# Sums and differences stored side by side in groups of four images, with matching loads and output, and the poles' rows loaded over 128 partitions

## The chip, the cores and the metric

The kernel runs on one core of a Trainium2 chip. The metric is device time in microseconds for one launch. The core has a matrix engine (TensorE, in the profile PE, with its weight loads as PEld), a vector engine (DVE), a scalar engine (ACT), a general engine (POOL) and a synchronisation engine (SP), which here issues nearly all transfers. Transfers between the on-chip memory and DRAM are carried out by 16 DMA engines.

## The reference

The input `x` has 16 images of 16 channels, 256 by 256, in float32. Two layers follow each other, each adding its result to its input:

```python
    # --- layer 0 (conv_preact) ---
    x = x + _L0_conv_ref(_gn(x), L0_conv_weight)
    # --- layer 1 (conv_preact) ---
    x = x + _L1_conv_ref(_gn(x), L1_conv_ty, L1_conv_tx, L1_conv_weights_pole1, L1_conv_weights_pole2, L1_conv_weights_residue)
    return x
```

`_gn` is a normalisation over 8 groups of two channels. Layer 0 is a circular 3 by 3 convolution of the 16 channels, which the reference writes with Fourier transforms. Layer 1 is a product in the Fourier domain with weights built from poles and residues, followed by two inverses:

```python
        alpha = jnp.fft.fft2(x, axes=(-2, -1))
        ...
        A = 1.0 / (omega1[:, None, None, None] - weights_pole1[None])
        Bm = 1.0 / (omega2[:, None, None, None] - weights_pole2[None])
        S = jnp.einsum('ikpq,oikp,xikq->oxik', weights_residue, A, Bm)
        output_residue1 = jnp.einsum('biox,oxik->bkox', alpha, S)
        C = jnp.einsum('biox,oikp->bikpx', alpha, A)
        D = jnp.einsum('bikpx,xikq->bikpq', C, Bm)
        output_residue2 = jnp.einsum('bikpq,ikpq->bkpq', D, weights_residue)
        x1 = jnp.fft.ifft2(output_residue1, s=(Ny, Nx), axes=(-2, -1)).real
        ...
        return x1 + x2 / Nx / Ny
```

`x2` is the transient: exponentials of the poles along both axes, weighted with `output_residue2`.

## The kernel before

The work is done in four stages, one after the other, with two tensors between them in DRAM that matter here: `v`, the result of layer 0, and the spectra. `v` is not kept as rows but as sums and differences of mirrored rows: for each row y of the upper half and its mirror image 255 - y, `vD[b][0]` holds the sum and `vD[b][1]` the difference, as 128 half rows by 16 channels by 256 columns, one tensor for each of the 16 images.

*Convolution* (lines 280 to 322). One image is 24 steps of `conv(g)`, and 384 steps follow each other. A step issues 16 matmuls of 32 by 32 weights. Six steps make a unit `u`, a quarter of an image: the accumulators of rows `r` 0 and 1 (upper half) are evicted by ACT at its last step (line 309), those of the mirrored rows, `r` 2 and 3, three steps later, each pair into a buffer `vt` of 4 KB per partition, of which there are six. Two steps on, `mirror` (line 259) forms the sum on DVE into `vsum` (two buffers, line 261) and the difference on POOL in place (line 264), and puts on lists what follows: ACT squares both for the statistics of layer 1 (line 272), and SP stores them (line 319), the sum's two halves at steps +4 and +5 and the difference's at +6 and +7 counted from the second eviction. A store has 256 KB, in runs of 1 KB. The rows of `x` are loaded two images ahead (line 123), in parts, on the same SP queue, and DVE takes their moments (line 179).

Between these steps the tables of layer 1 are made, one `yield` per step, by the generators `make_coef`, `make_poles`, `make_hat(0)`, `make_hat(1)` and `make_c`. `make_poles` computes seven quantities for all poles and writes each as 16 equal rows of 1024 numbers into `hD`. `make_hat` (line 419) needs five of them in all 128 partitions, in two halves of 512 numbers for each of two sides, four sets in all. It loads a set with eight transfers (line 439), each of five quantities from the 16 rows of `hD` to 16 partitions, waits six steps, and then ACT squares two of them (lines 452, 453), before POOL, DVE and PE go on.

*Transform* (lines 726 to 895). For each channel `i` and each group of four images from `b0`, `load_v` (line 726) reads sums and differences of the four images into a tile `s` of 2 by 4 by 256 numbers in each of 128 partitions, with one transfer per image; `fold` mirrors once more along x on DVE and POOL; PE transforms along y (lines 762, 770) and x (line 805). The loads run two groups ahead; the first group's is issued by POOL, the others by SP.

*Mixing* (lines 898 to 1228) reads the spectra `aD`, multiplies with the weights, and writes `yD`. It does not touch `v`.

*Inverse* (lines 1231 to 1426). 64 units of one channel `k` and four images. `load_v` (line 1281) reads the same parts of `v` again into `vl` (two buffers), one transfer per image; `combine` (POOL, line 1301) prepares the spectrum `yk`; PE goes along x (line 1337) and y (lines 1361, 1362); DVE writes the result into `r`. One unit later `put_out` (line 1368) adds half of `vl` to `r`, forms sum (line 1372) and difference (line 1373) of the two halves, which are the rows of the upper half and their mirror images, and stores each as one transfer for four images (line 1375).

Every transfer issued by SP waits until the one eight places before it on SP has landed, since eight semaphores are used in turn.

Of the kernel before, what the change touches and what calls it, by code (L numbers as in the profile page):

```python
# [9 lines left out]
FP = mybir.dt.float32  # L10
AF = mybir.ActivationFunctionType
ALU = mybir.AluOpType
# [4 lines left out]
B = 16  # L17
C = 16
N = 256
P = 128  # L20
# [4 lines left out]
def conv_then_laplace_kernel(ctx: ExitStack, tc: tile.TileContext, a: dict, out: bass.AP):  # L25
# [15 lines left out]
    nc = tc.nc  # L41
    x = a["x"]
# [22 lines left out]

    vD = [dp.tile([2, P, C, N], FP, name=f"vD{b}", tag=f"vD{b}") for b in range(B)]
    aD = dp.tile([P, 2 * C, N * B], FP, name="aD", tag="aD")
# [39 lines left out]
    p1 = ExitStack()  # L107
    wp = p1.enter_context(tc.tile_pool(name="conv_w", bufs=1))
    xp = p1.enter_context(tc.tile_pool(name="xt", bufs=5))
    vp = p1.enter_context(tc.tile_pool(name="vt", bufs=6))  # L110
    fp = p1.enter_context(tc.tile_pool(name="v_sums", bufs=2))
    jp = p1.enter_context(tc.tile_pool(name="junk", bufs=1))
# [145 lines left out]

    def mirror(g, b, u, lo, hi):
        both = fp.tile([P, 2, 2, N], FP, name="vsum", tag="vsum")  # L260
        nc.vector.scalar_tensor_tensor(  # L261
            both, lo, 1.0, hi, ALU.mult, ALU.add, accum_out=sums[:, b, u : u + 1]
        )
        nc.gpsimd.tensor_tensor(lo, lo, hi, ALU.subtract)  # L264
        folded.extend((g + 4 + 2 * j + r, b, u, j, t, r) for j, t in enumerate((both, lo)) for r in range(2))
        squared.append((g + 5, lambda: square(both, 4 + 2 * u, b, bias=shift2[:, b : b + 1])))
        squared.append((g + 7, lambda: square(lo, 5 + 2 * u, b)))

    def square(t, col, b, **by):

        junk = jp.tile([P, 4 * N], FP, name="junk", tag="junk")
        nc.scalar.activation(
            junk,
            t.rearrange("p r j x -> p (r j x)"),
            AF.Square,
            accum_out=sums[:, b, col : col + 1],
            **by,
        )

    def conv(g):  # L280
# [20 lines left out]
        for r in (0, 1) if g % 6 == 5 else (2, 3) if g % 6 == 2 else ():  # L301
            at = g if r < 2 else g - 3
            if not 0 <= at < 24 * B:
                continue
            b, u = at // 24, at // 6 % 4
            if r % 2 == 0:
                vt = vp.tile([P, 2, 2, N], FP, name="vt", tag="vt")
                acc["v", r // 2] = vt
            nc.scalar.activation(vt[:, r % 2], acc[r], AF.Identity, bias=ready[b][1])  # L309
            if r == 3:  # L310
                later.append((g + 2, lambda g=g, b=b, u=u, lo=acc["v", 0], hi=vt: mirror(g, b, u, lo, hi)))
        while later and (later[0][0] <= g or g >= 24 * B + 2):
# [3 lines left out]
        while folded and (folded[0][0] <= g or g >= 24 * B + 2):  # L316
            _, b, u, j, t, r = folded.pop(0)
            y = 64 * r + 16 * u
            nc.sync.dma_start(
                out=vD[b][j, y : y + 16].rearrange("(t y) c x -> (y c) t x", t=2),  # L320
                in_=t[:, r],
            )
# [96 lines left out]
    def make_hat(side):  # L419
# [12 lines left out]
        n = C * C * 2  # L432
        for half in range(2):
# [3 lines left out]
            at = slice(half * n, half * n + n)  # L437
            for p0 in range(0, P, 16):
                nc.sync.dma_start(
                    out=five[p0 : p0 + 16, 0:5],  # L440
                    in_=hD[0:5, side, :, at].rearrange("j a n -> a j n"),
                )
# [283 lines left out]
    def load_v(i, b0, eng=nc.sync):  # L726
        s = sp.tile([P, 2, 4, N], FP, name="s", tag="s")
        for j in range(4):
            eng.dma_start(
                out=s[:, :, j], in_=vD[b0 + j][:, :, i, :].rearrange("h y x -> y h x")  # L730
            )
        return s

# [547 lines left out]
    def load_v(k, b0):  # L1281
        vl = vp.tile([P, 2, 4, N], FP, name="vl", tag="vl")
        for j in range(4):
            nc.sync.dma_start(
                out=vl[:, :, j], in_=vD[b0 + j][:, :, k, :].rearrange("h y x -> y h x")
            )
        return vl
# [80 lines left out]
    def put_out(k, b0, r, vl):  # L1368

        nc.vector.scalar_tensor_tensor(r, vl, 0.5, r, ALU.mult, ALU.add)  # L1370
        ol = op.tile([P, 2, 4, N], FP, name="ol", tag="ol")
        nc.vector.tensor_tensor(ol[:, 0], r[:, 0], r[:, 1], ALU.add)
        nc.vector.tensor_tensor(ol[:, 1], r[:, 0], r[:, 1], ALU.subtract)
        for h in range(2):
            nc.sync.dma_start(
                out=out[k, b0 : b0 + 4, h].rearrange("b y x -> y b x"), in_=ol[:, h]
            )

# [23 lines left out]
    for n, (k, b0) in enumerate(units):  # L1402
# [7 lines left out]
        if n + 1 < len(units):  # L1410
# [4 lines left out]
            load_ahead(n + 1)  # L1415
        r = rp.tile([P, 2, 4, N], FP, name="r", tag="r")
        for j in range(4):
            pt = along_x(u_now[:, j])
            if last is not None:
                along_y(*last)  # L1420
            if j == 0 and n:
                put_out(*done)
            last = (ey_now[:, j], hs[:, j], pt, r[:, :, j], begun[j])
        done = (k, b0, r, v_now)
# [160 lines left out]
```

## Time and profile before

| | |
|---|---|
| median of 6 runs | 2675.11 us (2671.88 to 2684.48) |
| the profiled execution | 2671.88 us, span 2669.8 us |
| PE, PEld busy | 2485.9 us (93%), 1872.1 us (70%) |
| DVE busy | 1988.4 us (74%) |
| ACT busy | 1447.8 us (54%) |
| POOL busy | 1311.1 us (49%) |
| moved by DMA | 653.17 MB, mean 245 GB/s |
| packets | 476827, of them 426998 under 2 KB |
| issues: stores of v | 256 of 256 KB |
| issues: loads of v | 256 and 256 of 256 KB |
| issues: output | 128 of 512 KB |
| issues: poles' rows | 32 of 160 KB |

The span runs from the first to the last instruction. Busy times of engines overlap, so they don't add up to it. A share of busy time is a mean over four stages with different limits. The granted clock is the share of full speed at which TensorE was allowed to run; the DMA share is the mean busy share of the 16 DMA engines, and in a short window it can come out a little above 1. In a row of the timeline, what stands in brackets is how long the engine was idle before the instruction, and what ended that.

### The profile page before, as it was taken

To read this page: it belongs to the slowest core of one execution; us is meant where nothing else is said; L and a number is where in the kernel's file an instruction comes from. 1 tells how busy PE (TensorE), PEld (TensorE's weight loads), DVE (VectorE), ACT (ScalarE), POOL (GpSimd) and SP (SyncE) were. 2 spreads that over 40 slices of the span, in tenths; PEclk is the share of its full clock that TensorE was granted. 3 is DMA by queue.
4 is the path that set the end of the run, shared out by engine and by line. 5 is a ranking of instruction groups with operands and counts; after the bars stand their busy time and mean duration, and the time that the engine had idled before them with its cause. 6 is when DMAs were issued, how large, how long until landed. Compare 5 with 4: busy or idle time off the path is not lost.

```text
span 2669.8 us, 84449 instructions
## 1 busy us (share of the span) xinstructions
PE 2485.9 (93%) x35314; PEld 1872.1 (70%) x35314; DVE 1988.4 (74%) x3805; ACT 1447.8 (54%) x2726; POOL 1311.1 (49%) x1182
## 2 busy tenths in 40 slices
PE   5888999879999999997999999999699999999998
PEld 2454444457777777774877777788588888888887
DVE  7767688748888888887777778787366666766666
ACT  2565566566666666664666666666244444444443
POOL 1333368343333333333566755766546565555653
PEclk9999999989999999997999999999899999999999
DMA  7898979765656655664777777777889998898985
GB/s 273 276 277 277 285 254 307 259 207 174 217 202 229 237 211 200 237 237 149 216 223 225 225 222 223 219 226 221 243 274 296 285 289 284 282 292 280 298 277 180
DMA packets 476827, 653.17 MB, mean 245 GB/s; under 512 B 51062, under 2 KB 426998, under 8 KB 466592
## 3 DMA queue, kind: packets, MB, share of 16 engines
q1 hardware_dynamic: 475376, 640.58, 74.7%
q8 instruction: 278, 4.55, 0.7%
q0 software_dynamic: 928, 3.02, 0.4%
q10 hardware_dynamic: 144, 4.19, 0.4%
q14 instruction: 101, 0.83, 0.1%
HBM read 368.15 MB, written 280.36 MB: 243 GB/s over the span
## 4 chain that ended last, share of the span: by engine, by line
PE 55%; DMA 17%; DVE 14%; SPq 6%; ACT 3%; issue 3%; POOL 2%; ACTq 0%; DVEq 0%; POOLq 0%
PE ps_conv L294 11%; PE ps_y L762 9%; PE ps_y L770 8%; PE ps_mix L1094 7%; DMA yk<-yD 6%; DMA yD<-yt 6%; PE ps_x L805 4%; PE ps_p L1337 3%; PE ps_f L1361 3%; PE ps_f L1362 3%; DVE r L1370 3%; SPq L1108 3%; DMA out_y<-ol 3%; PE ps_s L1012 2%; DVE xst L179 2%
## 5 line engine op out<-in xcount | busy, mean ns | idle before, releaser
L1094 PE MATMUL ps_mix<-abd,sg 128*64 128x128 f32 x8192 | 480.1, 275 | 40.3 <-ACT yt L1207 29.4
L1094 PEld LDWEIGHTS ps_mix<-abd,sg 128*64 128x64 f32 x8192 | 446.2, 137 | 97.4 <-ACT yt L1207 54.7
L1301 POOL TENSOR_TENSOR u<-yk 128x512 f32<-128x512 f32 (+1 forms) x268 | 345.6, 1320 | 307.0 <-PE ps_p L1337 200.8
L294 PE MATMUL ps_conv<-xt,wc 32*32 32x512 f32 x12288 | 447.9, 612 | 46.8 <-issue 36.0
L294 PEld LDWEIGHTS ps_conv<-xt,wc 32*32 32x32 f32 x12288 | 249.4, 104 | 233.6 <-issue 146.6
L778 ACT ACTIVATE t<-ps_y,vmr 128x384 f32<-128x384 f32 x512 | 297.5, 581 | 162.9 <-PE ps_y L770 162.8
L1028 DVE STREAM_SHUFFLE sg<-ps_s 128x512 f32<-128x512 f32 (+1 forms) x264 | 326.0, 1325 | 0.0
L762 PE MATMUL ps_y<-tabE,vq 128*128 128x256 f32 x1024 | 313.5, 388 | 13.4 <-DVE vq L751 11.9
L264 POOL TENSOR_TENSOR vt<-vt 128x1024 f32<-128x1024 f32 x64 | 151.7, 2370 | 324.9 <-DVE vsum L261 256.4
L770 PE MATMUL ps_y<-tabO,vq 128*128 128x256 f32 x1024 | 306.0, 381 | 0.0
L1337 PEld LDWEIGHTS ps_p<-inv,u 128*128 128x128 f32 x2048 | 265.9, 193 | 50.4 <-issue 25.1
L1361 PE MATMUL ps_f<-pt,inv 128*128 128x256 f32 x1008 | 300.8, 380 | 0.0
L1362 PE MATMUL ps_f<-hs,ey 128*128 128x256 f32 x1008 | 299.8, 379 | 0.0
L1365 DVE TENSOR_TENSOR r<-ps_f,q 128x256 f32<-128x256 f32 x256 | 107.1, 419 | 252.9 <-ACT q L1364 252.9
L1337 PE MATMUL ps_p<-inv,u 128*128 128x128 f32 x2048 | 279.3, 280 | 13.3 <-POOL u L1305 13.1
L1207 ACT COPY yt<-ps_mix 128x512 f32<-128x512 f32 x352 | 191.1, 593 | 156.8 <-DMA yD<-yt 105.8
L309 ACT ACTIVATE vt<-ps_conv,xq 128x512 f32<-128x512 f32 x256 | 162.1, 683 | 167.6 <-PE ps_conv L294 167.4
L762 PEld LDWEIGHTS ps_y<-tabE,vq 128*128 128x128 f32 x1024 | 189.7, 191 | 89.9 <-ACT q L818 50.3
L1364 ACT COPY q<-ps_f 128x256 f32<-128x256 f32 x256 | 95.4, 373 | 288.8 <-PE ps_f L1362 283.8
L750 POOL TENSOR_TENSOR vq<-vf 128x512 f32<-128x512 f32 x64 | 81.5, 1273 | 293.4 <-DVE vf L754 276.5
L1339 ACT COPY pt<-ps_p 128x512 f32<-128x512 f32 x256 | 150.2, 587 | 136.4 <-PE ps_p L1337 132.0
L770 PEld LDWEIGHTS ps_y<-tabO,vq 128*128 128x128 f32 x1024 | 195.7, 191 | 27.0
(239 smaller groups left out, 4062.5 us busy)
## 6 DMA issues: line engine op xcount, KB each, us to landing
yD<-yt SPq DMA_DIRECT2D x512, 128.0 KB, 3.5
vl<-vD SPq DMA_DIRECT2D x256, 256.0 KB, 3.9
out_y<-ol SPq DMA_DIRECT2D x128, 512.0 KB, 9.6
s<-vD SPq DMA_DIRECT2D x252, 256.0 KB, 5.8
aD<-spec SPq DMA_DIRECT2D x15, 4096.0 KB, 13.5
yk<-yD SPq DMA_DIRECT2D x60, 1024.0 KB, 8.5
xt<-in_x SPq DMA_DIRECT2D x64, 645.0 KB, 5.9
xt<-in_x SPq DMA_DIRECT2D x64, 516.0 KB, 6.9
```

Source lines behind the costliest of these rows:

```text
L294: nc.tensor.matmul(acc[r][32 * c : 32 * c + 32], lhsT=ready[b][0][rows, phase, tap], rhs=halves[b][u // 2][rows, q : q + 5 : 4, 2 - tap : ...
L309: nc.scalar.activation(vt[:, r % 2], acc[r], AF.Identity, bias=ready[b][1])
L762: nc.tensor.matmul(ps[:, 0:N], lhsT=vf[:, xo, 0, j], rhs=tabE[:, 0 : i + 2 : i + 1], start=True, stop=False, skip_group_check=True,)
L770: nc.tensor.matmul(ps[:, P : P + N], lhsT=vf[:, xo, 1, j], rhs=tabO[:, i : C + 1 : C - i], start=False, stop=True, skip_group_check=True,)
L778: nc.scalar.activation(t[:, xo, j].rearrange("p l n -> p (l n)"), ps[:, 0:384], AF.Copy, scale=vmr[:, 0, b0 + j, i : i + 1],)
L1028: nc.vector.stream_shuffle(to[..., C + k : C + k + 2], src, swap)
L1094: nc.tensor.matmul(ps[64 * t : 64 * t + 64, j], lhsT=sg[:, f : f + 2].rearrange("p f m -> p (f m)"), rhs=abd[jq][:, :, 2 * t + cc, 2 * jj ...
L1207: (nc.vector.tensor_copy if m >= (2 if late else 3) else nc.scalar.copy)(o, src)
L1301: nc.gpsimd.tensor_tensor(u[:, :, j].rearrange("p b (c n) -> p c b n", c=8), in0, in1, o)
L1337: nc.tensor.matmul(ps[:, at], lhsT=u[:, n], rhs=tab, start=True, stop=True)
L1361: nc.tensor.matmul(ps[:, e], lhsT=tab, rhs=pt[:, e], start=True, stop=False)
L1362: nc.tensor.matmul(ps[:, e], lhsT=ey[:, e], rhs=hs, start=False, stop=True)
```

## The change

Three layouts change, and what is computed stays the same.

1. `v` in DRAM becomes one tensor for four images, with sum and difference of a row next to each other: 128 half rows, 16 channels, 4 images, 2, 256 columns. On chip, sum and difference of a unit share one buffer `pair` (three of 8 KB), the mirrored rows have buffers `far` (two of 4 KB), and ACT evicts the upper rows directly into the difference's place in `pair`. A unit is stored by two transfers of 512 KB in runs of 2 KB, at steps +7 and +8. The loads of the transform and the inverse take two images in one transfer, 4 KB in a row.
2. The output is laid out in the same way, and the host turns it back. `put_out` stores two images with both halves in one transfer.
3. A set of the poles' rows is loaded by five transfers, one for each quantity, each to all 128 partitions; the source is read eight times over.

```diff
-    vD = [dp.tile([2, P, C, N], FP, name=f"vD{b}", tag=f"vD{b}") for b in range(B)]
+    vD = [dp.tile([P, C, 4, 2, N], FP, name=f"vD{b}", tag=f"vD{b}") for b in range(B // 4)]
...
-    vp = p1.enter_context(tc.tile_pool(name="vt", bufs=6))
-    fp = p1.enter_context(tc.tile_pool(name="v_sums", bufs=2))
+    vp = p1.enter_context(tc.tile_pool(name="v_pair", bufs=3))
+    fp = p1.enter_context(tc.tile_pool(name="v_far", bufs=2))
...
-    def mirror(g, b, u, lo, hi):
-        both = fp.tile([P, 2, 2, N], FP, name="vsum", tag="vsum")
+    def mirror(g, b, u, pair, hi):
+        both, lo = pair[:, :, :, 0], pair[:, :, :, 1]
         nc.vector.scalar_tensor_tensor(
             both, lo, 1.0, hi, ALU.mult, ALU.add, accum_out=sums[:, b, u : u + 1]
         )
         nc.gpsimd.tensor_tensor(lo, lo, hi, ALU.subtract)
-        folded.extend((g + 4 + 2 * j + r, b, u, j, t, r) for j, t in enumerate((both, lo)) for r in range(2))
+        folded.extend((g + 7 + r, b, u, pair, r) for r in range(2))
...
-            if r % 2 == 0:
-                vt = vp.tile([P, 2, 2, N], FP, name="vt", tag="vt")
-                acc["v", r // 2] = vt
-            nc.scalar.activation(vt[:, r % 2], acc[r], AF.Identity, bias=ready[b][1])
+            if r == 0:
+                pair = vp.tile([P, 2, 2, 2, N], FP, name="pair", tag="pair")
+                acc["v", 0] = pair, pair[:, :, :, 1]
+            elif r == 2:
+                far = fp.tile([P, 2, 2, N], FP, name="far", tag="far")
+                acc["v", 1] = far, far
+            to = acc["v", r // 2][1]
+            nc.scalar.activation(to[:, r % 2], acc[r], AF.Identity, bias=ready[b][1])
...
-            _, b, u, j, t, r = folded.pop(0)
+            _, b, u, pair, r = folded.pop(0)
             y = 64 * r + 16 * u
             nc.sync.dma_start(
-                out=vD[b][j, y : y + 16].rearrange("(t y) c x -> (y c) t x", t=2),
-                in_=t[:, r],
+                out=vD[b // 4][y : y + 16, :, b % 4].rearrange("(t y) c h x -> (y c) t (h x)", t=2),
+                in_=pair[:, r].rearrange("p t h x -> p t (h x)"),
             )
...
-            for p0 in range(0, P, 16):
+            for j in range(5):
                 nc.sync.dma_start(
-                    out=five[p0 : p0 + 16, 0:5],
-                    in_=hD[0:5, side, :, at].rearrange("j a n -> a j n"),
+                    out=five[:, j],
+                    in_=hD[j, side, :, at].unsqueeze(0).to_broadcast([8, 16, n]),
                 )
...
     def load_v(i, b0, eng=nc.sync):
-        s = sp.tile([P, 2, 4, N], FP, name="s", tag="s")
-        for j in range(4):
-            eng.dma_start(
-                out=s[:, :, j], in_=vD[b0 + j][:, :, i, :].rearrange("h y x -> y h x")
-            )
-        return s
+        s = sp.tile([P, 4, 2, N], FP, name="s", tag="s")
+        for j in range(0, 4, 2):
+            eng.dma_start(out=s[:, j : j + 2], in_=vD[b0 // 4][:, i, j : j + 2])
+        return s.rearrange("p b h x -> p h b x")
...
     def load_v(k, b0):
-        vl = vp.tile([P, 2, 4, N], FP, name="vl", tag="vl")
-        for j in range(4):
-            nc.sync.dma_start(
-                out=vl[:, :, j], in_=vD[b0 + j][:, :, k, :].rearrange("h y x -> y h x")
-            )
+        vl = vp.tile([P, 4, 2, N], FP, name="vl", tag="vl")
+        for j in range(0, 4, 2):
+            nc.sync.dma_start(out=vl[:, j : j + 2], in_=vD[b0 // 4][:, k, j : j + 2])
         return vl
...
         nc.vector.scalar_tensor_tensor(r, vl, 0.5, r, ALU.mult, ALU.add)
-        ol = op.tile([P, 2, 4, N], FP, name="ol", tag="ol")
-        nc.vector.tensor_tensor(ol[:, 0], r[:, 0], r[:, 1], ALU.add)
-        nc.vector.tensor_tensor(ol[:, 1], r[:, 0], r[:, 1], ALU.subtract)
-        for h in range(2):
-            nc.sync.dma_start(
-                out=out[k, b0 : b0 + 4, h].rearrange("b y x -> y b x"), in_=ol[:, h]
-            )
+        ol = op.tile([P, 4, 2, N], FP, name="ol", tag="ol")
+        nc.vector.tensor_tensor(ol[:, :, 0], r[:, :, 0], r[:, :, 1], ALU.add)
+        nc.vector.tensor_tensor(ol[:, :, 1], r[:, :, 0], r[:, :, 1], ALU.subtract)
+        for j in range(0, 4, 2):
+            nc.sync.dma_start(out=out[k, b0 // 4, :, j : j + 2], in_=ol[:, j : j + 2])
...
-        r = rp.tile([P, 2, 4, N], FP, name="r", tag="r")
+        r = rp.tile([P, 4, 2, N], FP, name="r", tag="r")
...
-    out = nc.dram_tensor("out_y", (C, B, 2, P, N), FP, kind="ExternalOutput").ap()
+    out = nc.dram_tensor("out_y", (C, B // 4, P, 4, 2, N), FP, kind="ExternalOutput").ap()
```

More of the change, by code (lines that the diff above doesn't have):

```diff
@@ L269, in square @@
     def square(t, col, b, **by):
-        junk = jp.tile([P, 4 * N], FP, name="junk", tag="junk")
+        junk = jp.tile([P, 4, N], FP, name="junk", tag="junk")
         nc.scalar.activation(
             junk,
-            t.rearrange("p r j x -> p (r j x)"),
+            t.rearrange("p r j x -> p (r j) x"),
             AF.Square,
@@ L305, in conv @@
             b, u = at // 24, at // 6 % 4
-            if r % 2 == 0:
-                vt = vp.tile([P, 2, 2, N], FP, name="vt", tag="vt")
-                acc["v", r // 2] = vt
-            nc.scalar.activation(vt[:, r % 2], acc[r], AF.Identity, bias=ready[b][1])
+            if r == 0:
[6 more added lines that the diff above has]
+            nc.scalar.activation(to[:, r % 2], acc[r], AF.Identity, bias=ready[b][1])
             if r == 3:
-                later.append((g + 2, lambda g=g, b=b, u=u, lo=acc["v", 0], hi=vt: mirror(g, b, u, lo, hi)))
+                later.append((g + 2, lambda g=g, b=b, u=u, pair=acc["v", 0][0], hi=to: mirror(g, b, u, pair, hi)))
         while later and (later[0][0] <= g or g >= 24 * B + 2):
@@ L1422, in conv_then_laplace_kernel @@
                 put_out(*done)
-            last = (ey_now[:, j], hs[:, j], pt, r[:, :, j], begun[j])
+            last = (ey_now[:, j], hs[:, j], pt, r[:, j], begun[j])
         done = (k, b0, r, v_now)
@@ L1582 @@
     r = run_bass_kernel_spmd(nc, [arrays], core_ids=[0])
-    y = r.results[0]["out_y"].transpose(1, 0, 2, 3, 4)
+    y = r.results[0]["out_y"].transpose(1, 3, 0, 4, 2, 5).reshape(B, C, 2, P, N)
     return np.concatenate([y[:, :, 0], y[:, :, 1, ::-1]], 2)
```

## The prediction

> **What bounds the kernel now.** I read the busy time by stage first, since the kernel is four stages with different limits: convolution (0 to 590 us), transform (to 1200), mixing (to 1895), inverse (to the end). Columns: span, then busy us and instruction count of PE, PEld, DVE, ACT, POOL; granted clock, DMA share, GB/s.
>
> ```profile
> core 0: us, PE busy (x) PEld busy (x) DVE busy (x) ACT busy (x) POOL busy (x), PEclk, DMA share, GB/s
> 0.00:590.00 590.00, 503.35 (x12646) 274.10 (x12646) 426.16 (x898) 335.41 (x602) 250.22 (x192) 0.97 0.82 268
> 590.00:1200.00 610.00, 605.39 (x4008) 437.12 (x4009) 518.61 (x1181) 365.60 (x629) 219.74 (x280) 0.99 0.61 217
> 1200.00:1895.00 695.00, 636.06 (x12556) 524.65 (x12555) 529.20 (x1023) 424.30 (x732) 404.47 (x307) 0.98 0.73 216
> ...
> 2002.00:2660.00 658.00, 653.19 (x5418) 561.74 (x5416) 451.65 (x626) 285.73 (x678) 374.80 (x334) 1.00 0.88 279
> ```
>
> In the transform and the inverse TensorE is busy for 605 of 610 and 653 of 658 us at full clock: a cheaper transfer is worth nothing there, as long as it stays hidden. The mixing stage moves none of the tensors changed here. Of the stages that are touched, the convolution alone leaves PE much idle time, 87 us, some 33 of them in its first 67 us, before the first weights and while they come. So next I looked inside it, for the places where PE stops, and the largest stand right behind the loads of the poles' rows (line 439). Timeline around the second set:
>
> ```profile
> 131.87 3.64 SPq L439 DMA_DIRECT2D s_h<-hD  x8
> ...
> 144.66 0.72 ACT L452 ACTIVATE s_den<-s_h,s_kcol 128x512 f32<-128x512 f32 x1 [2.93 <-DMA s_h<-hD]
> ...
> 144.68 6.23 PE L294 MATMUL ps_conv<-xt,wc 32*32 32x512 f32 x98 [4.57 <-issue]
> ```
>
> Eight loads of 160 KB need from 131.87 to about 144.66, 12.8 us, and PE starts again as they end. The same stretch by short windows, and last a stretch of convolution without loads:
>
> ```profile
> 136.00:140.00 4.00, 4.00 (x122) 2.51 (x103) 0.82 (x2) 2.96 (x5) 2.13 (x1) 1.00 1.08 123
> 140.00:142.00 2.00, 0.12 (x1) 0.00 (x0) 1.27 (x3) 1.74 (x4) 0.00 (x0) 1.00 1.11 126
> 142.00:145.00 3.00, 0.32 (x16) 0.28 (x31) 1.17 (x2) 0.34 (x1) 2.34 (x1) 0.80 1.03 281
> 145.00:150.00 5.00, 5.00 (x98) 2.06 (x67) 3.20 (x5) 0.91 (x2) 1.27 (x1) 0.50 1.06 394
> ...
> 530.00:565.00 35.00, 35.00 (x1072) 24.30 (x1051) 17.67 (x41) 25.10 (x44) 11.87 (x5) 1.00 0.45 149
> ```
>
> All 16 queues are full (1.08) and move 123 GB/s; once the loads are through, the same share moves 394. PE runs dry and then gets half its clock for 5 us. Why PE stops the profile calls only "issue", waiting for nothing it shows; by its place it is the crawl. Last, the sizes and landing times of the transfers in question, which all land within 10 us (columns: count, KB each, median us to landing), and from the timeline the two places where a transfer lies open, the start of the transform and the end:
>
> ```profile
> vl<-vD SPq DMA_DIRECT2D x256, 256.0 KB, 3.9
> out_y<-ol SPq DMA_DIRECT2D x128, 512.0 KB, 9.6
> s<-vD SPq DMA_DIRECT2D x252, 256.0 KB, 5.8
> ...
> vD<-vsum SPq DMA_DIRECT2D x128, 256.0 KB, 5.6
> ```
>
> ```profile
> 580.79 3.16 POOL L729 DMA_DIRECT2D s<-vD  x4
> ...
> 2664.03 1.22 DVE L1373 TENSOR_TENSOR ol<-r 128x1024 f32<-128x1024 f32 x1
> ```
>
> **The poles' rows.** Four sets of eight loads, each to 16 partitions, become four sets of five, each to all 128 from a source read eight times. Bytes stay at 1.31 MB a set. What a set costs PE: the convolution alone runs 1072 matmuls in 35 us, 30.6 a us. From 136 to 150 there are 122+1+16+98 = 237 in place of 428, 6.2 us lost. The same count gives 325 of 490 from 208 to 224 (5.4 us) and 375 of 520 from 278 to 295 (4.7 us). At the first set the timeline has gaps of 0.98 and 0.33 us. Together 17.6 us, the most that this edit can bring: it comes if the set moves at the 394 GB/s of the row at 145 us, 3.3 us. At the other end the copies share queues so badly that the crawl doubles: 17.6 us more. The destinations are now those of `s` and `vl`, 128 partitions, which the kernel loads all the time with no such crawl, so the value lies near the good end; since the source stays 16 rows read by several queues at once I take 11 of the 17.6, in proportion a set in 6.9 us, (12.8 - 6.9)/(12.8 - 3.3): **-11 us**. ACT, blocked at line 452 for 2.93 us in the second set, is covered by the same number. Three issues a set fewer on SP (0.45 us each, 3.64/8) are hidden.
>
> The Trainium skill speaks against this edit ("DMA: Bandwidth & Descriptors", Rules for kernel authors): an outermost zero-stride dimension of c copies confines a DMA to at most c engines, here 8 of 16. With that page's 27 GiB/s per engine (Specifications), 8 engines would need, as an estimate, 5.7 us a set and not 3.3, and the edit would bring at most 13 us by the same proportion, were the 8 not in each other's way as well. No run here shows yet which it is.
>
> **Stores of v (line 319).** 256 of 256 KB in 1 KB runs become 128 of 512 KB in 2 KB runs. The arithmetic on DVE, POOL and ACT keeps its order and sizes and only steps over gaps; lines 1372 and 743 already work on such parts at the usual pace, so nothing is charged. SP now waits 102 us for the sums and 86 us for the differences, with the loads of x queued behind; issued at steps +7 and +8, when both are done, the stores no longer block. That is hidden mostly, because x is loaded two images ahead; DVE waits for x 16.3 us in all. The chain holds two waits for a buffer behind a store, 6.34 us at 419.7 and 4.28 at 455.9, but PE's own gaps there are below 1.6 us. I take **-1 us**, between -5 (a third of PE's 17 us idle from 340 to 530) and the loss priced below.
>
> **Loads of v.** Pairs of images, 4 KB runs: half the issues. In the transform and the inverse this is hidden under PE. Exposed is the first one: POOL takes 3.16 us to issue four, two at 0.79 each take 1.58: **-1.6 us** (0 if PE, which starts at 593, follows the landing alone; -3 if that shortens too). `vl` must be there 9.1 us after it is issued (from 2201.0 to line 1370 at 2210.1) and lands in 3.9; if it became late, each of 64 units would pay. At the inverse's start, where PE is idle for 19 of 107 us (1895 to 2002), it waits for POOL and `yk`; two issues fewer on SP, 0.9 us, only bring the next groups' `yk` forward: nothing.
>
> The skill has a second objection (same page, Latency and other measured facts, row pitch): rows a large power of two apart slow copies, 207 GB/s at 512 KiB against 214 with a padded pitch. Rows of v now lie 128 KB apart. The trace shows 512 KB apart without harm: `aD` is written so, 4096 KB landing in 13.5 us, 310 GB/s. By row and rule alike the charge is nothing.
>
> **Output.** Each of the two stores needs both halves of the result. At the end the first goes out after 2665.25 and not 1.2 us sooner, beside the sum of line 1373; then 512 KB more lie open: 1.3 us at 394 GB/s, 1.9 at 279. **+1.5 us** (0 to 2). Before the end it is hidden.
>
> Sum: -11 -1 -1.6 +1.5 = **-12.1 us**. The profiled execution took 2671.88 us (span 2669.8), so it would take 2659.8; the median of the runs, 2675.11, is 3.2 higher: **2663 us**. Ends: -17.6 -5 -3 +0 = -25.6 gives 2649.5.
>
> **Rivals.**
> *The crawl stays* (the loads reach all partitions, but a few queues or parts of the memory still carry them). For it: the source is still 16 rows, and eight copies of a row are asked for together. Against it: `s_t<-in_tx`, one row to 128 partitions, 128 KB, lands in 3.3 us. Then -1 -1.6 +1.5: **2674 us**, no change.
> *The joint buffer is held too long* (slower). Sum and difference share one of three buffers, freed only when the last store lands. First evicted at step 0, the second store issues at step 11, and ACT wants the buffer at step 18. A step takes 1.5 us (images 36.1 us apart, 24 steps), so a landing may take some 10 us before ACT waits, and three steps (4.5 us) more before PSUM stops PE: it decides from 14.5 us on. The row for 512 KB stores is 9.6 us; before, the difference had 256 KB and 4.4 us. At 15 us PE would lose 0.5 us in each of 64 units, 32 us: 2663 + 32 = **2695 us**. No transfer of 512 KB has so late a median here.
> *The inverse becomes bound by transfers* (slower). There DMA is at 0.88; a unit of 11.4 us moves about 3.3 MB, `vl` a third. If `vl` took twice its time, 0.88 + 0.27 = 1.15: +1.7 us in 58 units, about 100 us, 2763. Against it: 8 KB runs 512 KB apart (`yk`) land 1 MB in 8.5 us.
>
> **Chances.** Forecast 0.56 (its own range 2650 to 2667), crawl stays 0.20, buffer 0.17, inverse 0.04, other losses 0.03. About 0.3%, 8 us, is what this kernel's runs can tell from nothing. So faster 0.56, same 0.20, slower 0.24. The range goes from 2650, the good end, to 2684, which takes in the unchanged case and the light part of the buffer's: some 2 in 10 lie outside.
>
> **What would show it.** Right: no PE gap above 2 us behind the five loads of a set, GB/s above 250 there, and the convolution's end some 12 us sooner; inverse and transform as long as before; the last landing 1.5 us later after line 1373. Wrong: windows at 1.0 share and 130 GB/s again (crawl stays); ACT's eviction waiting for the store of `pair` (buffer); PE idle in the inverse with POOL or DVE waiting for `vl`. A convolution shorter with those loads as slow as ever would make the prediction right for the wrong reason.

## The result, and the profile after

The changed kernel takes 2693.21 us (median of 21 runs, 2686.21 to 2700.42); the kernel before, run beside it, 2676.81 (47 runs). The ratio is 1.006 with a 95% interval of 1.005 to 1.007: some 16 us slower, where 2663 and 12 us faster were forecast. The profiled execution has a span of 2694.1 us. Of the runs below, one execution each of stores_apart (its profiled one, so that only its times are used), poles_alone and own_image_16 ran at a granted clock of 0.75 to 0.86 in place of 0.98 and is left out of the ratios.

The windows by stage, cut at the same events as before (the convolution 21 us later, and so on):

```profile
core 0: us, PE busy (x) PEld busy (x) DVE busy (x) ACT busy (x) POOL busy (x), PEclk, DMA share, GB/s
0.00:611.00 611.00, 507.86 (x12646) 272.41 (x12646) 427.30 (x898) 335.27 (x602) 248.48 (x190) 0.97 0.77 258
611.00:1221.00 610.00, 605.75 (x4009) 437.46 (x4010) 518.99 (x1181) 365.74 (x629) 219.69 (x280) 0.99 0.57 218
1221.00:1922.00 701.00, 642.46 (x12552) 532.17 (x12551) 527.29 (x1023) 424.55 (x731) 406.29 (x308) 0.96 0.72 213
2030.00:2684.00 654.00, 651.82 (x5416) 561.56 (x5415) 447.25 (x627) 285.03 (x678) 393.48 (x333) 1.00 0.81 279
```

The transform takes 610 us as before and the inverse is as full of TensorE as before, at a lower DMA share. The mixing stage is longer by 6 to 7 us, at a granted clock of 0.96 in place of 0.98. Its code is the same, and in the profiles of the kernels in the table below it lasts 679 to 690 us from the transform's last matmul to its own, without order; so that is taken for scatter. From there to the end they take 767 to 779 us, and here 774 in place of 777. Each profile is one execution, so a few us in one of them decide nothing. What is left is the convolution: its last matmul starts at 600.9 us in place of 580.6. TensorE stands idle there for 77.3 us in place of 61.3, and loses 15.4 us in place of 11.9 to half clock after pauses. The group of its matmuls on the page (busy us and mean ns, then idle time before them and what ended most of it) says the same, first before and then after the change:

```profile
L294 PE MATMUL ps_conv<-xt,wc 32*32 32x512 f32 x12288 | 447.9, 612 | 46.8 <-issue 36.0
L294 PE MATMUL ps_conv<-xt,wc 32*32 32x512 f32 x12288 | 449.8, 612 | 62.0 <-issue 56.0
```

And the second set of the poles' rows, which was to move at over 250 GB/s with no gap behind it, in short windows of the changed kernel:

```profile
138.00:142.00 4.00, 4.00 (x141) 3.00 (x134) 1.75 (x4) 3.21 (x6) 2.38 (x1) 1.00 0.87 257
142.00:145.00 3.00, 2.64 (x79) 1.23 (x69) 1.34 (x3) 2.30 (x4) 0.03 (x1) 1.00 0.90 207
145.00:148.00 3.00, 2.85 (x94) 1.34 (x63) 1.09 (x2) 1.02 (x2) 2.35 (x1) 1.00 1.02 252
148.00:152.00 4.00, 1.07 (x32) 0.48 (x33) 0.00 (x0) 1.10 (x3) 1.26 (x1) 0.85 1.04 411
```

The bytes move faster than the 123 GB/s of before, but these are now the set, the stores and x together, and TensorE still falls dry at 148.

**What "issue" is.** The trace keeps each DMA packet. Among them are those of the queue that carries instructions:

```profile
q8 instruction: 278, 4.55, 0.7%
```

(Packets, MB, share of 16 engines.) That is 16 KB each. Over TensorE's 70628 matmuls and weight loads the 4.55 MB come to 64 bytes for each, so I take the queue to be TensorE's; by that estimate a packet holds 128 matmuls and as many weight loads, 4.2 us of work at 30.6 matmuls a us. I laid TensorE's 28 gaps of over 0.8 us between 60 us and the convolution's end beside them. 22 gaps (39.6 us) end 1.2 to 1.7 us after such a packet has ended; with a packet every 5.7 us on average, chance would put about one in ten there. So I take it that TensorE had no instructions. Four (12.2 us) end 0.1 us after an image's weights are written (line 237): TensorE waited for them. The kernel before has 18 gaps of the first kind (30.3 us) and three of the second (5.5 us). One of the second kind, in the changed kernel's timeline:

```profile
176.60 0.42 DVE L237 SCALAR_TENSOR_TENSOR wc<-wband,xq,imask 128x192 f32<-128x192 f32 x1
...
177.12 1.94 PE L294 MATMUL ps_conv<-xt,wc 32*32 32x512 f32 x21 [3.02 <-issue]
```

So the page's one word covers two causes: instructions that come late, and weights that do. Behind the weights stand the statistics of x, and DVE waits for rows of x for 16.9 us from 60 to 600 us, 6.65 at the longest (11.9 and 3.6 before); that these waits made the weights late is not shown.

### The profile page after: what moved, and what is told of

Read it like the earlier page. It is cut to its first block, busy times and chain, and to the rows that moved or that the text cites. A ratio compares the mean times of both kernels' runs of the same rounds, so it can differ in the third digit from the quotient of the medians.

```text
span 2694.1 us, 83862 instructions
## 1 busy us (share of the span) xinstructions
PE 2496.6 (93%) x35314; PEld 1878.6 (70%) x35314; DVE 1983.4 (74%) x3805; ACT 1447.5 (54%) x2726; POOL 1329.7 (49%) x1180
## 3 DMA queue, kind: packets, MB, share of 16 engines
q8 instruction: 278, 4.55, 0.7%
## 4 chain that ended last, share of the span: by engine, by line
PE 61%; DMA 6%; SPq 3%; DVE 3%; ACT 2%; POOL 1%; issue 1%; ACTq 0%; DVEq 0%; POOLq 0%
PE ps_mix L1096 9%; PE ps_y L764 9%; PE ps_p L1337 9%; PE ps_y L772 8%; PE ps_f L1361 8%; PE ps_f L1362 8%; DMA yD<-yt 5%; PE ps_x L807 4%; PE ps_s L1014 2%; SPq L1110 2%; PE ps_h L1321 2%; PE psd L792 1%; ACT yt L1209 1%; DVE sg L1030 1%; SPq L1083 1%
## 5 line engine op out<-in xcount | busy, mean ns | idle before, releaser
L1096 PE MATMUL ps_mix<-abd,sg 128*64 128x128 f32 x8192 | 487.7, 278 | 39.8 <-ACT yt L1209 26.4
L1096 PEld LDWEIGHTS ps_mix<-abd,sg 128*64 128x64 f32 x8192 | 454.5, 139 | 95.9 <-ACT yt L1209 57.8
L1301 POOL TENSOR_TENSOR u<-yk 128x512 f32<-128x512 f32 (+1 forms) x268 | 353.7, 1352 | 285.2 <-PE ps_p L1337 218.6
L764 PE MATMUL ps_y<-tabE,vq 128*128 128x256 f32 x1024 | 313.5, 388 | 13.8 <-DVE vq L753 12.2
L264 POOL TENSOR_TENSOR pair<-pair,far 128x1024 f32<-128x1024 f32 x64 | 151.6, 2369 | 350.3 <-DVE pair L261 315.4
L1029 ACT ACTIVATE sg<-ps_s,mcol 128x512 f32<-128x512 f32 (+1 forms) x264 | 168.0, 690 | 78.6 <-PE ps_s L1014 78.5
```

What stands on the lines that cost most here:

```text
L764: nc.tensor.matmul(ps[:, 0:N], lhsT=vf[:, xo, 0, j], rhs=tabE[:, 0 : i + 2 : i + 1], start=True, stop=False, skip_group_check=True,)
L1029: nc.scalar.activation(to[..., k : k + 2], src, AF.Copy, scale=nsgn)
L1096: nc.tensor.matmul(ps[64 * t : 64 * t + 64, j], lhsT=sg[:, f : f + 2].rearrange("p f m -> p (f m)"), rhs=abd[jq][:, :, 2 * t + cc, 2 * jj ...
L1301: nc.gpsimd.tensor_tensor(u[:, :, j].rearrange("p b (c n) -> p c b n", c=8), in0, in1, o)
```

## The experiments

Ratios are to the kernel before, run beside each kernel, with 95% intervals; the level of the kernel before moved between 2674 and 2678 us from session to session. "Dry" is TensorE's idle time in gaps over 0.8 us that end behind an instruction packet, "weights" behind line 237, "x" the mean time from the issue of a load of x to its last packet; idle time and these three are from one profiled execution, in the convolution.

| run | ratio | last conv. matmul | idle | dry | weights | x |
|---|---|---|---|---|---|---|
| before | 1 | 580.6 | 61.3 | 30.3 | 5.5 | 6.3 |
| changed | 1.006 [1.005, 1.007] | 600.9 | 77.3 | 39.6 | 12.2 | 7.8 |
| poles_undone | 1.0106 [1.0087, 1.0126] | 613.4 | 85.6 | 61.6 | 0.0 | 8.4 |
| poles_alone | 1.0009 [0.9994, 1.0024] | 585.6 | 65.6 | 29.7 | 12.3 | 6.6 |
| stores_apart | 1.0029 [1.0014, 1.0043] | | | | | |
| x_ahead | 1.0013 [0.9998, 1.0028] | 584.6 | 60.7 | 29.4 | 4.9 | 7.4 |
| poles_flat | 0.9957 [0.9942, 0.9973] | 573.9 | 59.9 | 32.4 | 3.3 | 6.3 |
| x_ahead_spread | 1.0009 [0.9996, 1.0023] | 586.1 | 61.4 | 33.0 | 0.0 | 7.1 |
| diffs_behind | 1.0017 [1.0005, 1.003] | 585.6 | 61.2 | 34.8 | 1.0 | 6.4 |
| before_16 | 0.9976 [0.9959, 0.9993] | 568.3 | 55.5 | 26.0 | 3.5 | 6.2 |
| after_16 | 1.0075 [1.0054, 1.0096] | 598.1 | 69.7 | 45.1 | 0.0 | 7.8 |
| x_ahead_16 | 1.0021 [1.0007, 1.0036] | 586.2 | 62.1 | 34.7 | 0.0 | 7.1 |
| apart_16 | 1.0034 [1.0021, 1.0046] | 595.1 | 71.2 | 44.3 | 4.0 | 6.7 |
| tiles_16 | 0.9959 [0.9941, 0.9977] | 571.6 | 57.5 | 34.9 | 1.8 | 6.3 |
| tiles_late_16 | 0.9931 [0.9912, 0.995] | 572.3 | 54.9 | 31.8 | 0.0 | 6.3 |
| layout_16 | 1.0029 [1.0013, 1.0045] | 587.3 | 71.7 | 47.8 | 1.3 | 6.7 |
| own_image | 1.0005 [0.9988, 1.0022] | 587.6 | 65.1 | 29.4 | 9.0 | 7.4 |
| own_image_16 | 0.998 [0.9965, 0.9995] | 575.2 | 61.4 | 30.4 | 4.7 | 7.2 |
| padded_16 | 0.9942 [0.9924, 0.996] | 573.1 | 58.5 | 31.4 | 3.1 | 7.1 |

### First: which part costs

*poles_undone*: the changed kernel with the old loads of the poles' rows (line 443); *poles_alone*: the kernel before with the new ones (the same edit, the other way).

```diff
-for j in range(5):
-    nc.sync.dma_start(out=five[:, j], in_=hD[j, side, :, at].unsqueeze(0).to_broadcast([8, 16, n]))
+for p0 in range(0, P, 16):
+    nc.sync.dma_start(out=five[p0 : p0 + 16, 0:5], in_=hD[0:5, side, :, at].rearrange("j a n -> a j n"))
```

> The changed kernel with the eight old loads of the poles' rows; all else as changed. Four theories stand. BUNCHING: the sums no longer leave while GpSimd still subtracts; both halves leave together just ahead of the loads of x, which land later by some 1.5 us (issue to last packet 7.8 us in place of 6.3), so the statistics and weights of later images come late and TensorE stands, 17 us in all; the poles' loads are a small gain on their own. POLES: the new five loads are what costs the 17 us. BUFFER: ACT waits for the joint buffer. SHAPE: the 2 KB runs at a pitch of 128 KB move more slowly. Bunching, buffer and shape expect this run 3 to 10 us above the changed kernel's 2693, 2696 to 2703; POLES expects about 2677.

> The kernel before with the five new loads of the poles' rows and nothing else changed. BUNCHING, BUFFER and SHAPE expect a gain of 3 to 10 us, 2667 to 2674, and TensorE's gaps of 4.6, 3.6 and 3.9 us behind the sets at 140, 216 and 285 us gone or halved. POLES expects 2690 to 2695.

The five new loads bring 12 us where they stand (1.0106 without, 1.006 with them) and nothing alone. POLES falls: they are not the loss. But the gain of 3 to 10 us that was expected of poles_alone is missing, and its trace shows why. Its second set:

```profile
131.28 3.10 SPq L439 DMA_DIRECT2D s_h<-hD  x5
...
142.56 0.72 ACT L452 ACTIVATE s_den<-s_h,s_kcol 128x512 f32<-128x512 f32 x1 [1.41 <-DMA s_h<-hD]
144.85 0.63 ACT L453 ACTIVATE s_den<-s_h 128x512 f32<-128x512 f32 x1 [1.58 <-DMA s_h<-hD]
...
147.70 4.79 PE L294 MATMUL ps_conv<-xt,wc 32*32 32x512 f32 x98 [3.88 <-issue]
```

ACT waits for the set's last rows until 144.85: 13.6 us from the first issue, against 12.8 before. The gap of TensorE behind it is 3.9 us, against 4.6.

*stores_apart*: sums and differences stored by themselves, as early as before, from the joint buffer into the new place.

```diff
-folded.extend((g + 7 + r, b, u, pair, r) for r in range(2))
+folded.extend((g + 4 + 2 * j + r, b, u, j, pair, r) for j in range(2) for r in range(2))
...
-out=vD[b // 4][y : y + 16, :, b % 4] ..., in_=pair[:, r] ...
+out=vD[b // 4][y : y + 16, :, b % 4, j] ..., in_=pair[:, r, :, j]
```

> The changed kernel, but sums and differences are stored by themselves again, at steps +4, +5 and +6, +7, four stores of 256 KB a unit in 1 KB runs, into the new layout and from the same joint buffer. BUNCHING expects the convolution to end some 20 us sooner than in the changed kernel, at 580 us in place of 601, and 2670 to 2678 in all; x lands 6.3 us after its issue again. POLES and BUFFER expect 2690 to 2696, since both are still there. SHAPE expects something between, as the runs are 1 KB again but at the new pitch.

*x_ahead*: the joint stores two steps later, behind the loads of x on SP's queue.

```diff
-folded.extend((g + 7 + r, b, u, pair, r) for r in range(2))
+folded.extend((g + 9 + r, b, u, pair, r) for r in range(2))
```

> The changed kernel with the joint stores two steps later (+9, +10), so that they stand behind the two loads of x of that unit on SP's queue and not ahead of them. BUNCHING expects x to be issued without the wait for GpSimd and to land sooner, and 2670 to 2685, unless the buffer, now held two steps longer, takes part of it. BUFFER expects a loss of 10 us or more on the changed kernel, above 2703, with ACT's evictions waiting for stores. POLES and SHAPE expect 2690 to 2696.

stores_apart gains back half of the loss and x_ahead most of it, which looked like the theory of bunching proved. But stores_apart, at 2682 us, lies above the range of BUNCHING and between the two levels, where SHAPE had put it. In x_ahead ACT waits 38.3 us for stores of the buffer and the kernel is still faster than the changed one, so BUFFER is weak: in the changed kernel that wait is 6.5 us in all.

(Waits of ACT from 60 to 600 us, first in x_ahead and then in the changed kernel; columns: us in total, times, longest.)

```profile
ACT pair L313 <- DMA vD<-pair: 38.3, 12, 5.7
```

```profile
ACT pair L313 <- DMA vD<-pair: 6.5, 3, 2.9
```

### Second: what a set of the poles' rows can bring

*poles_flat*: one load of the same bytes from 128 places.

```diff
-for p0 in range(0, P, 16):
-    nc.sync.dma_start(out=five[p0 : p0 + 16, 0:5], in_=hD[0:5, side, :, at].rearrange("j a n -> a j n"))
+nc.sync.dma_start(out=five[:, 0:5].rearrange("p j n -> p (j n)"),
+                  in_=x[0][:, 0:10].rearrange("p r w -> p (r w)")[:, 0 : 5 * n])
```

> The kernel before, with each set of the poles' rows replaced by one load of the same 1.31 MB from 128 separate rows of the input x, 10 KB runs (the tables then hold other numbers). It asks what a set that moves at full pace would bring. The prediction's reading, that the slow set stops TensorE, expects the gaps of 4.6, 3.6 and 3.9 us gone and a gain of 10 to 17 us, 2659 to 2667. The theory that those gaps come whenever some 1.3 MB stand in the queues ahead of the 16 KB instruction packets expects gaps of 2 to 4 us still there and 2672 to 2678.

It takes 0.9957, 11.5 us less (7 to 16 by the interval). So a set at full pace is worth some 11 us, where the prediction counted 17.6, and the gaps are not simply gone: the one behind the second set shrinks from 4.6 to 0.9 us, but two of 1.4 and 1.7 us follow it. TensorE's idle time falls by 1.4 us only; the time lost to half clock falls from 11.9 to 3.4.

*bursts*: three extra sets in the last two images of the kernel before, into spare buffers of x: the old loads, the flat one, the new ones. It was run once.

> The kernel before with three extra sets in the last image, where no x is loaded and no weights are awaited, into buffers that nobody reads: the eight old loads at about 528 us, one load of 10 KB runs from 128 places at about 543 us, the five new loads at about 555 us. FETCH, the theory that TensorE stops when its 16 KB instruction packet comes late behind slow transfers, expects a gap that ends 1.3 to 1.6 us behind such a packet: 3 to 5 us behind the old set, under 1.5 us behind the flat one, and 2 to 4 behind the new one if that too needs over 10 us. If the gaps need the awaited weights or x, no gap above 1 us shows at any of the three.

```profile
539.00:547.60 8.60, 8.46 (x219) 4.23 (x210) 4.93 (x11) 6.14 (x12) 2.37 (x1) 1.00 1.00 173
550.30:555.50 5.20, 4.31 (x144) 2.20 (x128) 2.06 (x13) 3.23 (x6) 0.00 (x0) 1.00 1.04 387
561.00:571.00 10.00, 10.00 (x318) 6.66 (x289) 2.47 (x4) 7.00 (x12) 2.52 (x2) 1.00 0.71 213
```

Each window covers one set. From the first packet to the last it takes 9.0 us for the old loads (all but five of 640 packets within 8.6), 5.0 for the flat one, 10.0 for the new ones. The old set fills all 16 queues (share 1.00) with packets of some 210 ns. The new set has packets of some 115 ns, 70 in a microsecond: 8 at a time. It leaves half the queues free (0.71, with stores beside it), but is itself slower. TensorE's gaps: none behind the old set, against the expected 3 to 5 us; 0.9 us at the flat one; 2.2 us behind the new one, after an instruction packet that took 2.4 us and the next 8 us later. A slow set does not stop TensorE every time.

*before_16*: 16 copies of 8 rows in place of 8 copies of 16 (the 16 rows of `hD` are equal).

```diff
-in_=hD[j, side, :, at].unsqueeze(0).to_broadcast([8, 16, n]),
+in_=hD[j, side, 0:8, at].unsqueeze(0).to_broadcast([16, 8, n]),
```

> The kernel before, its sets of the poles' rows read by five loads of 16 copies of 8 rows (all 16 rows hold the same numbers) in place of 8 copies of 16. The extra sets in the last image showed 8 queues busy at a time with the 8 copies, 70 packets a us of 115 ns, 10.1 us a set. ENGINES, the theory that the copies of the outer dimension set how many queues carry a load, expects some 16 busy, a set in 5 to 6 us and the gain of the flat set, 2662 to 2669. If the slow part is the source, the same rows read again and again, a set stays at 9 us or more and it takes 2674 to 2680.

```profile
130.00:135.50 5.50, 5.50 (x185) 3.92 (x180) 2.44 (x4) 5.20 (x9) 2.38 (x1) 1.00 0.90 240
```

Of the second set 604 of the 640 packets now start within these 5.5 us, some 120 a microsecond of 100 to 158 ns, some 14 at a time; the last ends 3 us later. The kernel takes 0.9976, 6.4 us less than before. The Trainium skill's rule ("DMA: Bandwidth & Descriptors", Rules for kernel authors), that an outermost dimension of c copies confines a load to at most c engines, agrees with these runs: 8 packets at a time with 8 copies, some 14 with 16.

### Third: the order of stores and x

*diffs_behind*: the kernel before, differences stored at +9 and +10. *x_ahead_spread*: x_ahead with the five loads of a set two steps apart.

```diff
-folded.extend((g + 4 + 2 * j + r, b, u, j, t, r) ...      (diffs_behind)
+folded.extend((g + 4 + 5 * j + r, b, u, j, t, r) ...
...
-for j in range(5):      (x_ahead_spread)
+for j in (3, 4, 0, 1, 2):
     nc.sync.dma_start(out=five[:, j], ...)
+    yield
+    yield
-for _ in range(6):
-    yield
```

> The kernel before with the differences' stores three steps later (+9, +10), so that the loads of x stand ahead of them on SP's queue and do not wait for GpSimd. BUNCHING expects x to land sooner than before and no loss: 2668 to 2677. If instead the order of x and the stores matters only through the buffers, ACT waits for the differences' buffer and it takes over 2680.

> The changed kernel with the joint stores two steps later, behind x (as in the run before that gave 2678), and the five loads of a set two steps apart rather than back to back. If what is left of the poles' price is the crowd of the five loads, the gaps of 2.0, 3.4 and 2.3 us at 142, 212 and 284 us go and it takes 2668 to 2674, below the kernel before. If their price does not depend on the crowd it takes 2676 to 2680.

Neither brings anything. Then all three forms of the changed kernel with the set of 16 copies: *after_16* (nothing else changed), *x_ahead_16*, *apart_16*.

> The changed kernel with the loads of 16 copies of 8 rows, all else as changed. ENGINES with BUNCHING expects 2680 to 2687: the set's part mended, the joint stores ahead of x still there, so slower than the kernel before. If the loss of the changed kernel was the set alone, it takes 2665 to 2675.

> The changed kernel with both mended: joint stores behind x (+9, +10) and the loads of 16 copies. If the two prices are separate and add up, 2665 to 2670, faster than the kernel before. If mending the order had already hidden the set's price, about 2678 again.

> The changed kernel with sums and differences stored by themselves again (+4, +5 and +6, +7) and the loads of 16 copies. What is left of the change is the layout of v, its loads in pairs, the joint buffer and the output. If these are worth nothing it takes what the kernel before with the 16 copies takes, within 5 us; x lands 6.3 us after its issue and TensorE's idle time in the convolution is near 61 us. If the joint buffer costs, ACT waits for stores and it takes over 5 us more than that one.

What gave 6.4 us in the kernel before gives nothing in any of these three (1.0075, 1.0021, 1.0034, against 1.006, 1.0013, 1.0029); after_16 and x_ahead_16 lie above all that was expected of them. And apart_16 is dry for 44.3 us although its stores leave as early as before, ACT waits for no store in it, and x lands in 6.7 us. Something was left in the changed kernel that neither the order nor the buffer explains.

### Fourth: the place of v in memory

*tiles_16*: apart_16 with v laid out and loaded as before. *tiles_late_16*: the same, but stored as late as in the changed kernel. *layout_16*: apart_16 with the buffers of the kernel before, so that only the place of v, its loads and the output are changed.

```diff
-vD = [dp.tile([P, C, 4, 2, N], ...) for b in range(B // 4)]      (tiles_16)
+vD = [dp.tile([2, P, C, N], ...) for b in range(B)]
...
-folded.extend((g + 4 + 2 * j + r, b, u, j, pair, r) for j in range(2) for r in range(2))      (tiles_late_16)
+folded.extend((g + 7 + r, b, u, j, pair, r) for r in range(2) for j in range(2))
```

> The run with stores apart and loads of 16 copies (1.0034 of the kernel before), with v in memory laid out as before (each image and half by itself, a store writes two stretches of 128 KB without gaps) and loaded by four loads as before; joint buffer and output stay as changed. SHAPE, now: 1 KB runs scattered 8 KB apart are what is left of the cost, and it takes what the kernel before with 16 copies takes, 0.9976, some 2668 to 2676. If the joint buffer or the output costs, it stays at 1.002 to 1.005, above 2681.

> As the run with v laid out as before, joint buffer and 16 copies, but the sums' stores wait for the differences' (all four of a unit at steps +7 and +8). This is the changed kernel's time of storing alone, at the old layout and the old 1 KB runs. BUNCHING expects 10 to 17 us over that run, with x landing about 1.5 us later. If the layout is the whole cost, it takes the same as that run within 3 us.

> The run with stores apart and loads of 16 copies (1.0034), with the buffers of the kernel before: six tiles for the halves and two for the sums, and no joint buffer; v in memory and its loads as changed. SHAPE expects 1.0034 again, within 0.002. If the joint buffer costs, it falls to 0.9976, that of the kernel before with 16 copies.

BUNCHING falls here: at the old place the late stores cost nothing (0.9931 against 0.9959). BUFFER falls: layout_16 has none of it and takes 1.0029, as apart_16 does with it (1.0034). What all kernels above 1.002 share is the place of v.

*own_image* and *own_image_16*: the changed kernel (and after_16) with a place for each image, sum and difference of a row side by side. *padded_16*: after_16 with 9 KB from run to run in place of 8.

```diff
-vD = [dp.tile([P, C, 4, 2, N], ...) for b in range(B // 4)]
+vD = [dp.tile([4, P, C, 2, N], ...) for b in range(B // 4)]      (own_image)
+vD = [dp.tile([P, C, 9, N], ...) for b in range(B // 4)]      (padded_16)
```

> The changed kernel with one thing undone: in memory each image of v has its own place again, both halves of a row side by side in 2 KB, so that a store writes two stretches of 256 KB without gaps; joint stores, their time, the paired loads, the five loads of 8 copies and the output stay as changed. SHAPE (scattered runs cost the convolution) expects at least the 17 us of the changed kernel's loss back: 2660 to 2676, TensorE idle for 55 to 65 us in the convolution in place of 77. BUNCHING expects the changed kernel's 1.006, about 2690, since the stores' time is the same.

> The same with loads of 16 copies. SHAPE expects 6 us or more below the run with 8 copies, at the level of the run with late stores at the old layout, 0.993, 2653 to 2664: then the joint stores cost nothing and the layout was the whole loss. If 512 KB joint stores cost by themselves, 2665 to 2680.

> The changed kernel with loads of 16 copies and 9 KB in place of 8 KB from one run of a store to the next (1 KB of each row unused). If the cost of the layout is the power of two between the runs, it goes: 2655 to 2668, as with each image in its own place. If it is that the runs are scattered at all, it stays: 2690 to 2700, as without the padding (1.0075).

The place alone (with loads of v in runs of 2 KB in place of 4) takes the changed kernel from 1.006 to 1.0005, and one unused kilobyte behind every eight takes after_16 from 1.0075 to 0.9942, some 35 us; in the two profiled executions 25 us of it lie in the convolution (it ends at 598.1 and 573.1), and the rest is no more than the scatter of the later stages. Its stores are as scattered as before, so it is the pitch of 8 KB and not the gaps. own_image_16, at 2671 us, lies in the range that stood for joint stores which cost by themselves; padded_16 has the same joint stores and takes 2659, so that is not the reason. The same stretch, 60 to 565 us, of after_16 and then of padded_16:

```profile
60.00:565.00 505.00, 450.18 (x11058) 235.75 (x11044) 367.63 (x732) 292.89 (x533) 225.67 (x176) 0.97 0.81 264
```

```profile
60.00:565.00 505.00, 461.05 (x11791) 249.64 (x11771) 375.88 (x752) 312.08 (x563) 237.04 (x180) 0.99 0.77 271
```

With the padding more is moved (271 GB/s) at a lower share of the queues' time (0.77), and TensorE runs 733 matmuls more. The packets say which are slow. Of the stores' packets from 330 to 520 us, where no set is loaded:

| kernel | bytes | from run to run | mean ns | over twice the median |
|---|---|---|---|---|
| before | 1 KB | 1 KB | 48.0 | 1.0% |
| tiles_late_16 | 1 KB | 1 KB | 48.5 | 0.9% |
| layout_16 | 1 KB | 8 KB | 52.5 | 5.2% |
| changed | 2 KB | 8 KB | 104.6 | 8.1% |
| after_16 | 2 KB | 8 KB | 103.2 | 7.4% |
| own_image | 2 KB | 2 KB | 91.1 | 1.6% |
| padded_16 | 2 KB | 9 KB | 92.1 | 1.8% |
| x_ahead | 2 KB | 8 KB | 86.6 | 0.8% |

From 540 to 568 us, where all but two of the loads of x are over, the stores of the changed kernel take 89.5 ns and those of own_image 87.6. So the 8 KB pitch hurts beside the loads of x, and x_ahead, whose stores leave behind them, is spared most of it: that is why it looked like a matter of order. Slow packets are not the whole account, though: in x_ahead_16 the stores' packets take 86.3 ns, 0.5% of them over twice the median, and it still takes 1.0021. ACT waits 28.7 us for stores there, which may be the reason; no run shows it.

## Why the prediction was wrong

**The bound.** That the convolution alone could move the end was right: its last matmul comes 20 us later, the last transfer adds 0.8 us, and the rest is within the scatter of the other stages. That the slow sets cost something was right too, but not how much: the sum of 17.6 us stands against 11.5 in poles_flat, where the gain came less from TensorE's idle time (1.4 us) than from its half clock (8.5 us). The sum was also counted wrongly, since a matmul under way at the border of two windows stands in both: as one window each, the three stretches have 220, 293 and 347 matmuls in place of 237, 325 and 375, and the sum would be 20 us, further off still.

**The poles' rows, -11 us.** This step failed at "the destinations are now those of `s` and `vl`, 128 partitions ... so the value lies near the good end" and its set in 6.9 us. The set took 13.6 us in poles_alone and 10.0 beside little else (bursts), and the edit by itself gave 1.0009: between 2 us gained and 6 lost. In the changed kernel, where the old loads cost more, the same edit is worth 12 us (1.0106 against 1.006), near the forecast, but not by a set of 6.9 us: there too ACT reads the last rows of the second set only 13 us after its first issue. The row of `s` and `vl` has 128 rows in its source; here the source had 8 copies, and the 8 decided. The skill's rule stood in the prediction with this very number, and I took the trace's nearest rows over it, although their sources had no copies. The rival "the crawl stays" had this part right for the edit alone. The prediction named 17.6 us lost as the other end of this term, and its range up to 2684 leaves that out.

**Stores of v, -1 us.** This is the step that decided the sign. In place of 1 us gained, 15 were lost in the changed kernel (own_image), 20 with 1 KB runs (apart_16 against tiles_16) and 35 with the better loads (after_16 against padded_16). I costed their number, their size, their run length and SP's waits, and did not ask where their runs go. A rule on row pitch stood two paragraphs on (the same page of the Trainium skill, Latency and other measured facts: rows a large power of two apart slow copies, and padding by a few KiB cures it), and was weighed for the loads alone, against `aD`, which is written in runs of 32 KB and not of 2. The figures of that rule begin at 512 KiB; these runs show the same cure at a pitch of 8 KB, with 1 KB, for stores that share the queues with loads.

**The buffer rival** gave the right time, 2695, by a wrong mechanism: ACT waited 6.5 us for stores and not 32, and layout_16, without the buffer, is as slow as apart_16 with it.

**Loads of v, -1.6 us.** The issue at the first load did shrink, but TensorE starts as late as before: 12.9 us after it (600.8 to 613.7) against 12.3. So the term was worth nothing, the end of its range at 0.

```profile
600.82 1.37 POOL L733 DMA_DIRECT2D s<-vD  x2
```

**Output, +1.5 us.** Right in kind, and 0.8 in size: from the start of line 1373 to the end 6.6 us against 5.8. **Inverse and transform** are as forecast, and the rival of an inverse bound by transfers did not come.

The terms as measured, +2, +15, +0.6 and +0.8, make 18 us, against 16.4 in the medians. The sum takes the poles' edit alone and the place of v last; in another order the two would come to other values, since the edit is worth 12 us beside the 8 KB pitch and nothing without it.

## What to carry to other kernels

Cost a change of layout by the addresses that one transfer touches, not only by its bytes and runs: 8 KB from run to run, beside other traffic, cost 15 to 35 us of 2675 here, and an unused kilobyte behind every eight cured it. Count the copies in the outermost dimension of a load: 8 copies kept 8 packets going at a time here, and 16 some 14. And an order of transfers that helps may only keep two streams apart that harm each other: change the place of one before believing in the order.

## What I had not expected

TensorE, with some 30 small matmuls a microsecond, runs out of instructions: 18 of the 22 gaps of the kernel before end 1.2 to 1.7 us behind a 16 KB instruction packet. This is shown by the timing alone; no run varied the packets by themselves, and bursts shows that a slow set need not cause it.

Five kernels that compute the same beat both: tiles_late_16 (0.9931), padded_16 (0.9942) and tiles_16 (0.9959) by 11 to 19 us against the kernel before, before_16 (0.9976) and own_image_16 (0.998) by 5 to 6.

Open are why the 16 copies bring 6 us with v in the old or in its own place and nothing at the 8 KB pitch, why own_image_16 (0.998) stays above padded_16 (0.9942), why before_16, whose convolution ends first of all in its profile, stays above tiles_16 and tiles_late_16, and what in the memory makes the 8 KB pitch slow beside x.
